# Softmax maxima as a row of the second pass's contraction, and two passes issued together in half steps of two strips

## The chip, the cores and the metric

The kernel runs on one core of one Trainium2 chip. The metric is the device time of one execution in microseconds, given as the median of several runs; a profiled execution gives the trace that the text reads. The engines are called as in the profile: PE (TensorE, with PEld for its weight loads), DVE (VectorE), ACT (ScalarE), POOL (GpSimd) and SP (the queue that issues most DMAs).

## The reference

Two layers of a network on 8 batches of 512 tokens with 256 channels, all in f32. The first layer is a multi-query attention (16 heads of 16 channels; one key head and one value head shared by all) and a top-64 mixture of 16 experts; the second is a linear attention and a coupled three-cycle network. Only the first attention matters here:

```python
q = (x @ Wq + bq).reshape(Bx, Tx, HEADS, HD)          # 16 heads of 16
k = (x @ Wk + bk)[:, :, None, :]                      # one head for all
v = (x @ Wv + bv)[:, :, None, :]
q, k = _apply_rope(q, ...), _apply_rope(k, ...)
att = jnp.einsum('bthd,bThd->bhtT', q, k) / math.sqrt(HD)
att = jnp.where(causal, -jnp.inf, att)
att = jax.nn.softmax(att, axis=-1)
out = jnp.einsum('bhtT,bThd->bthd', att, v).reshape(Bx, Tx, Cx)
return out @ Wo + bo
```

`x` there is a layer-normed and modulated input, and the result is added to `x` with a gate per batch and channel.

## The kernel before, in words

**Strips.** Keys and queries are kept transposed, channels on partitions. `qT[:, g]` holds 8 heads of 16 channels on 128 partitions (g = 0, 1). The 32 partitions 32j to 32j+31 are strip j: they hold two heads, an even one (p = 0) and an odd one (p = 1). `kT[:, p]` is the shared key, repeated on all partitions, with zeros on the 16 rows of the other head, so that one matmul over the 32 rows of strip j scores one head. Four strips lie in four row groups of PE, so four such matmuls can run at once, each into its own PSUM bank.

**Two passes.** Softmax needs the row maxima before it exponentiates. The first pass, `maxima(b)`, scores queries against keys with the queries on the output partitions: `L646` are the scores, `L654` adds a mask to each diagonal block of 128 x 128 by a bf16 matmul with the identity, and DVE takes maxima over stretches of 128 keys (`L668`, and `L661` where a bank holds blocks of two heads). The second pass, `heads_of(b)`, scores again with the keys on the output partitions: `L725` are the scores, `L733` subtracts the maxima by a further bf16 matmul, ACT exponentiates (`L740`) into `e`, POOL zeroes what lies above the diagonal (`L744`), and `values(n)` (`L710`) multiplies `e` with the values and a column of ones.

**Rounds.** Causal blocks of 512, 384, 256 and 128 columns are packed so that a round fills a 512-column bank: per g five rounds, `rounds`, of which three hold two blocks. A pass thus has ten rounds per batch, each of four strips, and takes or fills four banks in a round.

**The maxima's way.** `L675` reduces the partial maxima, `L679` and `L682` split them into three bf16 parts whose sum is the f32 number (three casts, two subtractions), four bf16 transposes (`L688`) turn them, ACT copies them to `mT` (`L691`). `minus` is a matrix of zeros and minus ones that picks, in the contraction of `L733`, the three rows that belong to a head.

**Order of the work.** The order on every engine is that in which the program emits instructions. `Steps.run()` goes round a set of lanes (Python generators) in order of rank, each lane emitting up to its next `yield`. A batch is one lane: `made_ready(b)` (norm, q, k, v, rope, transposes `L606`, `L616`), `maxima(b)`, `heads_of(b)`, `finished(b)` (transposes `L776` and `L791`, output product `L805`, norm, router logits `L831`). A new batch starts every 15 steps, so in the steady state four batches are under way: `finished(b)`, `heads_of(b+1)`, `maxima(b+2)`, `made_ready(b+3)`. A step holds one round of each pass, whole: first the four strips of the second pass, then the four of the first. The ranks are 0 for `finished`, 1 for `made_ready`, 2 for `heads_of`, 3 for `maxima`.

**Banks.** All PSUM tiles come from one pool of eight banks (`net.mm()`). A tile can be written when the reader of the bank's last tile is through. First-pass strips are released by DVE, second-pass strips by ACT, transposes and projections by either.

After the first attention come the experts (`experts_side`), the second layer's attention, and the coupled network; no line of theirs is changed, except that the second attention's lanes are counted in half steps too.

## Time and profile before

| what | value |
|---|---|
| median of 6 runs | 1192.93 us (1190.21 to 1195.59) |
| the profiled execution | 1191.77 us, its span 1190.0 us |
| mean granted clock of PE | 0.973 |
| PE busy | 1101.7 us (93%) |
| DVE busy | 711.1 us (60%) |
| ACT busy | 555.0 us (47%) |
| POOL busy | 498.2 us (42%) |
| matmuls of the first pass, L646 | 1024 records, 136.0 us busy |
| matmuls of the second pass, L725 | 1024 records, 106.5 us busy |
| mask, L654 | 512 records, 42.9 us busy |
| subtraction of the maxima, L733 | 512 records, 43.5 us busy |
| DVE maxima, L668 and L661 | 320, 198.4 us busy, 683 ns mean |
| exponentials, L740 | 320, 164.7 us busy, 604 ns mean |

An f32 matmul leaves two records (two loads, two matmuls), a bf16 one leaves one. PE's work is pipelined: the records of one line overlap those of the next, so that the busy times of lines add up to more than the span that they take; start-to-start distances are what one pays. A matmul that stands before the array and waits for a bank can count as busy. "Idle before" a group tells how long its engine stood still and whose work ended it.

### The profile page before, as it was taken

How to read it: one execution, taken by the hardware profiler on the slowest of the kernel's cores; microseconds unless marked ns; L12 is line 12 of the kernel's file. 1: busy time of each engine (PE TensorE's matmuls, PEld its weight loads, DVE VectorE, ACT ScalarE, POOL GpSimd, SP SyncE). 2: the span in 40 equal slices, each digit the busy share in tenths (PEclk: the TensorE clock that was granted, in tenths of full speed). 3: DMA queues.
4: the chain of work that ended last, by engine and by line, in shares of the span. 5: the costliest groups of instructions: out<-in, count | busy, mean ns of one | idle time of the engine just before them, and what ended most of it. 6: DMA issues, size and time to landing. Idle time of an engine off the chain costs nothing. (4 is left out here: it accounts for less than half of the span.)

```text
span 1190.0 us, 22170 instructions
## 1 busy us (share of the span) xinstructions
PE 1101.7 (93%) x8942; PEld 709.9 (60%) x8942; DVE 711.1 (60%) x1463; ACT 555.0 (47%) x1024; POOL 498.2 (42%) x539
## 2 busy tenths in 40 slices
PE   4879999999999999989898898799999988999996
PEld 3545666666666665478676776466666665444433
DVE  4967675767666666822652223666667655556765
ACT  2145656565656546724332344344444323555444
POOL 3022334344443424477787787355556444000000
PEclk8889999999999999999999999899999998999998
DMA  6200010000000001378758854400000000000202
GB/s 212 69 10 2 2 28 25 28 25 28 25 28 25 28 27 35 115 234 253 186 89 203 222 80 58 104 7 6 6 6 6 6 2 1 0 1 1 71 0 72
DMA packets 67975, 69.11 MB, mean 58 GB/s; under 512 B 10216, under 2 KB 64544, under 8 KB 67872
## 3 DMA queue, kind: packets, MB, share of 16 engines
q1 hardware_dynamic: 55024, 49.32, 13.3%
q0 software_dynamic: 12288, 16.79, 8.4%
q8 instruction: 71, 1.16, 0.4%
q10 hardware_dynamic: 560, 1.58, 0.4%
q14 instruction: 32, 0.26, 0.1%
HBM read 46.38 MB, written 21.01 MB: 57 GB/s over the span
## 5 line engine op out<-in xcount | busy, mean ns | idle before, releaser
L740 ACT ACTIVATE e<-mm 128x512 f32<-128x512 f32 x320 | 164.7, 604 | 103.1 <-PE mm L733 99.2
L668 DVE TENSOR_REDUCE pm<-mm 128x4 f32<-128x512 f32 x256 | 158.7, 683 | 84.1 <-PE mm L654 83.8
L744 POOL TENSOR_SCALAR_AFFINE_SELECT e<-e 128x512 f32<-128x512 f32 x128 | 80.3, 645 | 252.3 <-ACT e L740 252.3
L646 PE MATMUL mm<-kT,qT 32*128 32x128 f32 (+3 forms) x1024 | 136.0, 467 | 1.5 <-DVE o_tok L783 1.4
L1134 POOL DMA_INDIRECT xs<-y,slot x64 | 102.3, 1598 | 31.8 <-issue 13.3
L725 PE MATMUL mm<-qT,kT 32*128 32x128 f32 (+3 forms) x1024 | 106.5, 465 | 0.0
L646 PEld LDWEIGHTS mm<-kT,qT 32*128 32x128 f32 x1024 | 75.3, 189 | 45.0 <-DVE pm L668 10.9
L1642 PE MATMUL mm<-g,cn_w 128*128 128x512 f32 x192 | 98.3, 625 | 0.0
L710 PE MATMUL mm<-e,vaug 128*32 128x512 f32 (+3 forms) x1024 | 77.2, 436 | 3.9 <-POOL e L744 2.5
L725 PEld LDWEIGHTS mm<-qT,kT 32*128 32x128 f32 x1024 | 57.2, 184 | 26.6 <-issue 10.6
L1035 POOL DMA_INDIRECT tok<-xg,gidx x64 | 63.5, 993 | 19.1 <-issue 16.0
L1685 DVE SCALAR_TENSOR_TENSOR m<-th,slope,g 128x512 f32<-128x512 f32 x48 | 34.0, 747 | 58.8 <-ACT th L1678 58.8
L1462 POOL TENSOR_SCALAR_AFFINE_SELECT am<-am 128x1024 f32<-128x1024 f32 x32 | 44.1, 1381 | 55.5 <-ACT am L1460 55.5
L1111 PE MATMUL mm<-ew,hid 128*128 128x256 f32 x256 | 63.8, 394 | 1.0 <-ACT hid L1100 0.8
L1100 ACT ACTIVATE hid<-mm,eb 128x512 f32<-128x512 f32 x32 | 22.0, 686 | 91.2 <-PE mm L1091 91.2
L1098 DVE TENSOR_SCALAR hid<-mm,eb 128x512 f32<-128x512 f32 x32 | 24.0, 750 | 67.1 <-PE mm L1091 67.0
L1091 PE MATMUL mm<-hid,ew 128*128 128x256 f32 x256 | 61.5, 384 | 0.0
L1091 PE MATMUL mm<-tokT,ew 128*128 128x256 f32 x256 | 60.8, 380 | 0.1
L1116 DVE SCALAR_TENSOR_TENSOR y<-mm,eb,gb 128x512 f32<-128x512 f32 x32 | 23.9, 745 | 61.5 <-PE mm L1111 61.5
L1290 PE MATMUL mm<-hT,w1qkv 128*128 128x512 f32 x128 | 58.8, 604 | 0.0
L1642 PEld LDWEIGHTS mm<-g,cn_w 128*128 128x128 f32 x192 | 33.6, 195 | 41.7 <-issue 40.0
L1460 ACT COPY am<-mm 128x512 f32<-128x512 f32 x64 | 34.3, 591 | 44.5 <-PE mm L1448 30.7
(245 smaller groups left out, 2208.2 us busy)
## 6 DMA issues: line engine op xcount, KB each, us to landing
ew<-in_L_ffn_w SPq DMA_DIRECT2D x72, 256.0 KB, 5.9
x<-in_L_attn_x SPq DMA_DIRECT2D x8, 512.0 KB, 8.2
xs<-x SPq DMA_DIRECT2D x8, 512.0 KB, 4.9
xg<-xh SPq DMA_DIRECT2D x8, 512.0 KB, 4.1
x<-xs SPq DMA_DIRECT2D x8, 512.0 KB, 9.3
out<-res SPq DMA_DIRECT2D x16, 256.0 KB, 2.2
ga_row<-gate_a SPq DMA_DIRECT2D x16, 128.0 KB, 3.1
mod_row<-rows SPq DMA_DIRECT2D x16, 128.0 KB, 4.0
```

Source lines behind the costliest of these rows:

```text
L646: nc.tensor.matmul(strips[j][:, at : at + nk], qT[rows_of(j), g, i * P : (i + 1) * P], kT[rows_of(j), p, :nk], start=(n == 0), stop=False, ...
L668: nc.vector.tensor_reduce(pm[:, j, 2 * g + p, first : first + 4], strips[j].rearrange("q (a k) -> q a k", k=P), AX.X, ALU.max,)
L710: nc.tensor.matmul(av[32 * j : 32 * j + 32, c * P :], va[:, c, :], e[:, j, at : at + T - c * P], start=(a == 0), stop=(a == 3), skip_group ...
L725: nc.tensor.matmul(strips[j][:, at : at + T - c * P], kT[rows_of(j), p, c * P : (c + 1) * P], qT[rows_of(j), g, c * P :], start=(n == 0), ...
L740: nc.scalar.activation(e[:, j, :], strips[j], AF.Exp, scale=scale)
L744: nc.gpsimd.affine_select(out=own, in_=own, compare_op=ALU.is_ge, fill=0.0, base=0, pattern=[[0, 4], [1, P]], channel_multiplier=-1,)
L1035: self.net.nc.gpsimd.indirect_dma_start(out=tok[:, n, :], out_offset=None, in_=self.net.xg[half], in_offset=bass.IndirectOffsetOnAxis(ap=s ...
L1091: nc.tensor.matmul(ps[:, o * C : (o + 1) * C], w[i][n][:, k, o * P : (o + 1) * P], src[:, k, :], start=(k == 0), stop=(k == 1),)
L1111: nc.tensor.matmul(ps[:, n * C : (n + 1) * C], hid2[i][:, k, n * P : (n + 1) * P], w[i][2][:, k, :], start=(k == 0), stop=(k == 1),)
L1134: nc.gpsimd.indirect_dma_start(out=net.xs[2 * half + n], in_=y[i][:, n, :], in_offset=None, out_offset=bass.IndirectOffsetOnAxis(ap=self.s ...
L1290: nc.tensor.matmul(ps, w[:, k, n * P : (n + 1) * P], hT[:, k, :], start=(k == 0), stop=(k == 1))
L1642: nc.tensor.matmul(ps, w1[:, k, o * P : (o + 1) * P], g[k][bb], start=(k == 0), stop=(k == 1),)
```

## The change

Three things are changed together, in the first attention alone.

1. **The maxima become a row of the contraction.** Queries are kept once per head of a strip: `qT[g][:, p]` now has zeros on the 16 rows of the other head, as `kT[:, p]` has. On those rows `kT[:, p]` gets a minus one at the first of them (a bias of the ACT instruction that writes it). In the first pass this row meets a zero. Afterwards the maxima, in f32, are transposed (`L732` of the new kernel, eight f32 transposes in place of four in bf16) and added by DVE into that row of `qT[g][:, p]` (`L737`, four `scalar_tensor_tensor`). The second pass then needs no subtraction: `L733` of the old kernel is gone, and with it the bf16 parts, `mT` and its copy. `kT` and `qT` have two buffers instead of three.

2. **Masks of a bank are added by one matmul** instead of one per block (`hide`).

3. **Half steps.** A lane may yield a list of groups of matmuls instead of emitting them. `Steps.run()` collects these lists and emits them group by group: in one half step two strips of the second pass and two of the first, in different row groups, then the masks. Both passes walk the same list, `ORDER`, in which `None` is a place where the second pass does `values(n)` and the first nothing. All other lanes move every second half step. Batches start every 30 half steps.

Besides, the adds of the output bias and the two products with the modulation rows on POOL are split by tiles of 128 tokens, and `values(n)` is emitted in two halves.

```diff
     def run(self):
+        step = 0
         while self.starters or self.lanes:
             self.starters = [s for s in self.starters if next(s, self) is not self]
+            together = []
             for at in sorted(self.lanes, key=lambda at: at[:2]):
+                if step % at[3] != at[4] % at[3]:
+                    continue
                 self.now = at
-                if next(at[2], self) is self:
+                got = next(at[2], self)
+                if got is self:
                     self.lanes.remove(at)
+                elif got is not None:
+                    together.append((at, got))
+            for groups in itertools.zip_longest(*(got for _, got in together), fillvalue=()):
+                for issue in itertools.chain(*groups):
+                    issue()
+            for at, _ in together:
+                self.now = at
+                if next(at[2], self) is self:
+                    self.lanes.remove(at)
+            step += 1
...
-        kT = fp.tile([P, 2, T], F32, name="kT", bufs=3)
+        kT = fp.tile([P, 2, T], F32, name="kT", bufs=2)
...
         for p in range(2):
-            nc.scalar.activation(kT[:, p, :], ps, AF.Copy, scale=even_odd[:, p : p + 1])
+            nc.scalar.activation(
+                kT[:, p, :], ps, AF.Identity, bias=minus[:, 1 - p : 2 - p],
+                scale=even_odd[:, p : p + 1],
+            )
...
-            nc.scalar.copy(qT[:, g, :], ps)
+            q = fp.tile([P, 2, T], F32, name=f"qT{g}", bufs=2)
+            for p in range(2):
+                nc.scalar.activation(q[:, p, :], ps, AF.Copy, scale=even_odd[:, p : p + 1])
...
+    ORDER = (0, 1, 2, 3, None, 4, 5, None, 6, 7, 8, None, 9)
...
+            for js in ((0, 1), (2, 3)):
+                strips, groups = scores(g, blocks, js)
+                yield groups
+                for j in js:
...
         for i in range(NT):
-            nc.vector.tensor_reduce(mx[:, i], pm[:, :, :, blocks_of[i]], AX.X, ALU.max)
-        left = mx
-        for r in range(3):
-            part = m3[:, :, :, r : 12 : 3]
-            nc.vector.tensor_copy(part, left)
-            if r < 2:
-                rest = fp.tile([P, NT, 4, 4], F32, name=f"rest{r}")
-                nc.vector.tensor_tensor(rest, left, part, ALU.subtract)
-                left = rest
-            yield
-        mT = fp.tile([P, T], BF16, name="mT")
-        ps = net.mm(BF16)
-        for i in range(NT):
-            nc.tensor.transpose(
-                ps[:, i * P : (i + 1) * P], m3[:, i].rearrange("p j s -> p (j s)"), net.identb
-            )
-        nc.scalar.copy(mT, ps)
+            for p in range(2):
+                nc.vector.tensor_reduce(
+                    mx[:, i, :, :, 1 - p, 0],
+                    pm[:, :, p:4:2, blocks_of[i]].rearrange("q j g k -> q g j k"), AX.X, ALU.max,
+                )
+        yield
+        for g in range(2):
+            ps = net.mm()
+            for i in range(NT):
+                nc.tensor.transpose(
+                    ps[:, i * P : (i + 1) * P], mx[:, i, g].rearrange("q j p e -> q (j p e)"),
+                    net.ident,
+                )
+            for p in range(2):
+                nc.vector.scalar_tensor_tensor(
+                    qT[g][:, p, :], ps, even_odd[:, 1 - p : 2 - p], qT[g][:, p, :],
+                    ALU.mult, ALU.add,
+                )
+            yield
         yield
...
-                for p, a, at in blocks:
-                    c = chunk_of[a]
-                    for j in range(4):
-                        nc.tensor.matmul(
-                            strips[j][:, at : at + T - c * P],
-                            minus[rows_of(j), 2 * g + p, :], mT[rows_of(j), c * P :],
-                            start=False, stop=True, skip_group_check=True,
-                        )
...
+            for js in ((2, 3), (0, 1)):
+                strips, groups = scores(g, blocks, js)
+                yield groups
+                for j in js:
+                    nc.scalar.activation(e[:, j, :], strips[j], AF.Exp, scale=scale)
```

## The prediction

> **What bounds the kernel now.** I read the page's slices first, because the change touches only the first attention, and then its groups.

> ```profile
> PE   4879999999999999989898898799999988999996
> DVE  4967675767666666822652223666667655556765
> PEclk8889999999999999999999999899999998999998
> ```

> Slices of 29.75 us: from the fourth to the seventeenth TensorE is full while VectorE stands at 5 to 8 tenths. The transposes of the maxima (L688) begin at 69.0 for batch 0 and at 467.8 for batch 7, so seven batches pass in 398.8 us, 57.0 each. The windows view, cut at the period, repeats to a hundredth (columns: window, length, then busy time and count of PE, PEld, DVE, ACT, POOL, then clock):

> ```profile
> 234.00:292.50 58.50, 58.09 (x617) 36.29 (x617) 39.87 (x85) 33.64 (x65) 23.91 (x30) 1.00 0.09 27
> 292.50:351.00 58.50, 58.10 (x617) 36.30 (x617) 39.87 (x85) 33.64 (x65) 23.91 (x30) 1.00 0.08 27
> ```

> So a batch is 58.5 us of TensorE; VectorE and ScalarE have 18.6 and 24.9 us to spare, and the clock is full. But a waiting matmul counts as busy, so the timeline of TensorE decides how much of that is work:

> ```profile
> 301.57 0.40 PE L654 MATMUL mm<-maskb,identb 128*128 128x128 bf16 x4
> 301.90 1.22 PE L725 MATMUL mm<-qT,kT 32*128 32x384 f32 x16
> 302.87 0.46 PE L733 MATMUL mm<-mT,minus 32*128 32x384 bf16 x8
> ...
> 316.27 0.40 PE L654 MATMUL mm<-maskb,identb 128*128 128x128 bf16 x4
> 316.50 0.39 PE L791 MATMUL mm<-ident,o_tok 128*128 128x128 f32 x2
> ...
> 340.19 0.40 PE L733 MATMUL mm<-mT,minus 32*128 32x256 bf16 x8
> 340.40 2.03 PE L646 MATMUL mm<-kT,qT 32*128 32x512 f32 x8
> 342.37 0.40 PE L654 MATMUL mm<-maskb,identb 128*128 128x128 bf16 x4
> ```

> I count from start to start, since tails overlap. A round of the second pass (L725, four strips at once) takes 301.90 to 302.87 = 0.97 us. The same work in the first pass (L646) takes 340.40 to 342.37 = 1.97 here. The ten rounds of this batch take 1.20, 1.45, 2.15, 1.08, 2.09, 0.97, 1.08, 1.97, 1.97 and 2.36 us in the first pass, 16.3 in all, some 0.6 of it interleaved second-pass work, against 10.1 for the second pass: **5.6 us of waiting per batch**. It waits for banks that VectorE empties four at a time:

> ```profile
> 301.84 2.48 DVE L668 TENSOR_REDUCE pm<-mm 128x4 f32<-128x512 f32 x4 [0.65 <-PE mm L654]
> 307.91 2.48 DVE L668 TENSOR_REDUCE pm<-mm 128x4 f32<-128x512 f32 x4 [0.84 <-PE mm L654]
> ```

> Each reduction occupies VectorE 0.62 us; both lines start as soon as the mask matmuls are through.

> **The change, per batch of 58.5 us, TensorE first.**

> *Removed: the matmuls that subtract the maxima (L733).* 64 per batch. A round with one block has four, about 0.30 us; one with two blocks eight, 0.39 us (302.87 to the next start 303.26). 4 × 0.30 + 6 × 0.39 = **−3.6 us**. All on the path: TensorE is full.

> *Added: transposes of the maxima in f32.* Eight instead of four bf16 ones. Four f32 transposes take 0.50 (L776, as above a start-to-start distance), four bf16 ones 0.32 (L688, 296.57 to 296.89): 2 × 0.50 − 0.32 = **+0.7 us**.

> *Merged: mask matmuls.* 64 of 128 columns become 16 of 128 and 24 of 256, the same columns. Four of 128 take 0.23 (316.27 to 316.50), eight 0.46 (307.59 to 308.05): the cost is the columns, so **0**.

> *Moved: masks after every half step.* The mask uses the whole array, the scores 32-row strips. Four masks followed by another full-array job last 0.23, followed by strips 0.33 (301.57 to 301.90): a change of shape costs 0.10. Now there are 13 entries into strips per batch, after the change 20, and as many exits: 14 × 0.10 = at most 1.4; exits often cost nothing (324.08 to 325.05 is the bare 0.97), so between 0.7 and 1.4; I take **+1.3**. [...]

> *Pairing.* In the new order a half step issues two strips of the second pass (row groups 64 to 127, say) and two of the first (0 to 63), block by block with equal sizes, so four still run at once and scores keep 2 × 10 × 0.97.

> Without any waiting TensorE would need 58.5 − 5.6 − 3.6 + 0.7 + 1.3 = **51.3 us**.

> *VectorE.* Gone are three casts and two subtractions, 3 × 0.24 + 2 × 0.23 = 1.4. Added are four more small reductions (L675, four in 0.50: 0.4) and four 128x512 scalar_tensor_tensor from PSUM; the trace shows one of 0.75 (L1116), so 3.0. 39.9 − 1.4 + 3.4 = **41.9**. ScalarE: two more 0.58 copies, less mT's 0.5: 34.3. GpSimd's 2.36 us adds are cut in four; nobody waits for them. No DMA is added. kT and qT have two buffers instead of three: the new kT waits for the last second-pass round two batches back, behind exponentials that need the same matmuls, so 0.

> *What is left of the waiting.* Eight banks; a half step takes four and its side job one or two, so half step k+1 needs what VectorE released from k−1. A half step is TensorE about 1.25 (scores, two masks, a shape change), VectorE 1.24. Side jobs unbalance it in two places. Where BN statistics (1.0), cosd (1.43) and kd (0.6) fall on five half steps in a row, VectorE needs 5 × 1.24 + 3.0 = 9.2 against 6.3: some 2.5 us late even after the one half step of slack. At the start of a batch the last scalar_tensor_tensors, BN statistics (2.0) and four o_tok (4 × 0.63) make 1.4 us more. I take **3.9**, against 5.6 now; bounds 0 (VectorE's sum is 9.4 below TensorE's) and 7.2 (its bursts eat the whole gain).

> *The seam.* Both passes now walk the same list, so four half steps between batches hold no scores. The chain there: last mask, two reductions (1.45), wo_g and bo_g (0.94), eight small reductions (0.9), transposes (0.7), two scalar_tensor_tensors (1.5) = 5.5 us to the first usable queries. TensorE has meanwhile the k and q transposes, values(3), both transposes of maxima and the logits, 6 us. Cost 0.3, in the 3.9.

> Period: 51.3 + 3.9 = 55.2, **−3.3** (bounds −7.2 and 0). Seven such intervals, three of them without some lane, so I count 4 × 3.3 + 3 × 3.0 = **−22**.

> *Ends.* Batch 0's first pass runs alone, two strips at a time: a pair costs what four do, since a lone f32 matmul of 512 columns takes 2 × 0.51 (L1642, 98.3 us for 192). That is up to +9.7 of TensorE, but there VectorE is busy 27.6 of 31.5 us, so it is the bound: between 0 and +8, I take +2. Batch 7's second pass alone loses L733 (−3.6) and pairs only where no other matmul lies between half steps (up to +9.7): −3.6 to +6, taken +1. Together **+3**.

> Sum: −22 + 3 = −19. The profiled execution took 1191.8 (span 1190.0, 1.8 around it), 1.2 below the median of the six runs: 1172.8 on its scale, 1174 on the median's; as the later layers run the same instructions I leave them as they are and say 1173.

> **The rivals.**

> *The waits go (1147).* Two reductions at a time release banks every 1.24 instead of 2.48 us. Then 51.3 per batch: 7 × −7.2 + 3 = −47; allowing some residue, 1147 to 1158. For it: VectorE is only 82% full. Against: the two crowded places.

> *VectorE becomes the bound (1191).* All 7.2 are eaten: 1190 to 1196 with the ends. For it: the present 5.6 at 68% load; VectorE's load rises to 76%.

> *Slower: the seam is exposed (1210).* The place is the wait of the transposes of the maxima, which stand in TensorE's queue ahead of half of values(3) and the logits. If VectorE reaches the chain late, its 5.5 us lie open: +5.5 − 3.3 = 2.2 per batch, 15 in all, with the ends 1210. It decides from 3.3 us of idle TensorE per seam. The trace has such a place, batch 0, where nothing covers:

> ```profile
> 66.07 1.09 PE L606 MATMUL mm<-ident,kd 128*128 128x128 f32 x4 [5.24 <-DVE kd L594]
> ```

> and the windows view (first pair of numbers 4.00 us: TensorE busy; the last three: clock, DMA share, GB/s):

> ```profile
> 70.00:74.00 4.00, 4.00 (x23) 1.50 (x21) 0.00 (x0) 1.95 (x5) 0.00 (x0) 0.57 0.00 0
> ```

> 5.24 us idle, and then a granted clock of 0.57. [...] Against it: the 6 us of cover.

> *It does not pair (1309).* If strips of two passes did not overlap, scores would double: 20 × 0.97 = 19.4 more per batch, 136 in seven. Against: today's four are also separate instructions into separate banks.

> **Numbers.** Forecast 0.60 (1158 to 1186), waits gone 0.18, VectorE bound 0.10 (of this 0.03 faster, 0.04 same, 0.03 slower), seam 0.09, no pairing 0.03. Six runs spread over 0.45%, so about 0.3% (3.6 us) can be told from no change. Faster 0.60 + 0.18 + 0.03 = 0.81, same 0.04, slower 0.15. Range: from inside the second case to the top of the third, 1151 to 1191; outside lie the seam, no pairing and the lower part of the second case, 0.2.

> **What would show it.** Right: a period near 55 us; L733's successor absent; scores of both passes in mixed bursts of about 1 us; VectorE near 42 of 55; first-pass matmuls still waiting where cosd and kd fall; no half clock at the seams. Wrong: a period of 51 (waits gone) or 58 (VectorE at 90% around the reductions), TensorE idle over 3 us before the transposes of the maxima, or bursts of 2 us.

## The result, and the profile after

The changed kernel takes 1200.39 us (median of 20 runs, 1192.21 to 1203.92) against 1192.95 us (median of 46, 1189.54 to 1198.53): ratio 1.0047, interval 1.0033 to 1.006. It is slower by half a per cent, where a gain of 1.7% was forecast, and lies above the range. Within the changed kernel the time goes with the mean granted clock: four runs at 0.965 to 0.966 took 1192.2 to 1193.1 us, those at 0.954 to 0.956 took 1198.9 to 1203.9 us; no trace of any of the four was kept, so where they gain is not known. The profiled execution took 1198.88 us, span 1197.2, clock 0.956 (before: 0.973).

The page's slices (29.9 us each now), in the rows that were read before:

```profile
PE   4999999999999999979898999799999988999996
DVE  4577968586777777722552223666667655556765
PEclk8579999999999999999899999899999998999998
```

TensorE looks as full as before. The news is in the second and third digits of the last row, 5 and 7 where 8 and 8 stood, and in VectorE's second digit, 5 for 9. The middle of the first attention is better than before (windows view, cut at the new period; columns as above):

```profile
188.40:245.10 56.70, 56.55 (x535) 31.85 (x534) 42.23 (x88) 35.72 (x66) 25.70 (x39) 1.00 0.09 27
245.10:301.70 56.60, 56.45 (x534) 31.75 (x532) 42.12 (x88) 35.63 (x66) 25.70 (x39) 1.00 0.09 28
```

58.5 us per batch have become 56.65, with VectorE at 42.2 (41.9 forecast). Three stretches of the profiled spans, cut at the first and last score of the second pass (L725 before, L777 after), hold the whole difference:

| stretch | before | after | difference |
|---|---|---|---|
| start to the first score of the second pass | 70.4 | 89.4 | **+19.0** |
| from there to the last one | 428.8 | 414.5 | **-14.3** |
| from there to the end | 690.8 | 693.3 | +2.5 |

So a gain of the expected kind is there, and is lost again before the second pass has begun. There batch 0's first pass runs alone. The windows view of that place, before:

```profile
40.00:50.00 10.00, 10.00 (x101) 6.09 (x97) 9.65 (x18) 1.77 (x3) 0.00 (x0) 1.00 0.01 2
50.00:60.00 10.00, 10.00 (x89) 6.47 (x82) 9.83 (x26) 0.00 (x0) 0.82 (x1) 1.00 0.01 3
```

and after:

```profile
40.00:50.00 10.00, 10.00 (x38) 4.56 (x36) 5.38 (x10) 2.07 (x4) 1.55 (x4) 0.50 0.00 0
50.00:60.00 10.00, 10.00 (x46) 4.68 (x47) 5.01 (x13) 0.78 (x1) 0.00 (x0) 0.50 0.00 0
60.00:70.00 10.00, 10.00 (x32) 5.18 (x29) 5.57 (x12) 0.78 (x1) 0.00 (x0) 0.50 0.09 26
```

TensorE is busy all the time in both. Before, VectorE is at 9.65 and 9.83 of 10 at full clock: it is the bound, as the prediction had it. After, VectorE is half idle, and the clock stands at 0.50 without a break from 25 to 70 us. The timeline of TensorE after shows what runs at that clock:

```profile
47.87 2.08 PE L674 MATMUL mm<-kT,qT 32*128 32x512 f32 x4
49.88 0.39 PE L684 MATMUL mm<-maskb,identb 128*128 128x128 bf16 x2
50.20 2.08 PE L674 MATMUL mm<-kT,qT 32*128 32x512 f32 x4
52.21 0.39 PE L684 MATMUL mm<-maskb,identb 128*128 128x128 bf16 x2
```

A half step of two strips takes 2.33 us (47.87 to 50.20), of which VectorE uses two reductions (1.29 us, L717 from 50.20 on). Both kernels come to this place with a low clock (0.60 and 0.75 before, 0.50 and 0.50 after, in the windows from 25 and from 30 us), and in both TensorE has little to do from 20 to 35 us (busy 5.17 of 15.00 us before, 6.86 after). Before, it is at 1.00 from 40 us on, to the end of this pass. After, it opens only between 71 and 72 us (0.72 in the window of that microsecond, 0.50 in those ahead of it, 1.00 from 72 us on), towards the end of a long product over the whole array (L582: q, k and v of the next batch):

```profile
66.35 6.68 PE L582 MATMUL mm<-wqkv,hT 128*128 128x288 f32 x16
72.96 1.14 PE L674 MATMUL mm<-kT,qT 32*128 32x384 f32 x8
74.03 0.39 PE L684 MATMUL mm<-maskb,identb 128*128 128x256 bf16 x2
```

From then on the scores of the same two strips take 1.07 us (72.96 to 74.03) where they took 2.01 (47.87 to 49.88): twice the clock, half the time.

**The steady state after**, in the timeline of TensorE: a half step without waiting, then one that waits.

```profile
263.53 0.70 PE L777 MATMUL mm<-qT,kT 32*128 32x512 f32 x2
263.54 0.70 PE L674 MATMUL mm<-kT,qT 32*128 32x512 f32 x2
264.06 0.59 PE L777 MATMUL mm<-qT,kT 32*128 32x512 f32 x2
264.08 0.59 PE L674 MATMUL mm<-kT,qT 32*128 32x512 f32 x2
264.60 0.28 PE L684 MATMUL mm<-maskb,identb 128*128 128x128 bf16 x2
...
292.67 0.70 PE L777 MATMUL mm<-qT,kT 32*128 32x512 f32 x2
293.09 0.69 PE L674 MATMUL mm<-kT,qT 32*128 32x512 f32 x1
293.20 0.59 PE L777 MATMUL mm<-qT,kT 32*128 32x512 f32 x2
293.62 1.19 PE L674 MATMUL mm<-kT,qT 32*128 32x512 f32 x3
294.74 0.28 PE L684 MATMUL mm<-maskb,identb 128*128 128x128 bf16 x2
```

The first takes 263.53 to 264.60 = 1.07 us for two strips of each pass, so the passes do run together. The second takes 292.67 to 294.74 = 2.07: the second pass's strips go, the first pass's wait for banks that VectorE still holds. It is the half step that cosd delays, as the timeline of VectorE shows:

```profile
291.15 1.28 DVE L602 TENSOR_TENSOR cosd<-qkv,rope 128x1088 f32<-128x1088 f32 x1
292.35 2.48 DVE L710 TENSOR_REDUCE pm<-mm 128x4 f32<-128x512 f32 x4
```

kd runs on VectorE only at 296.56, and no half step waits behind it (the next one, at 298.54, takes 1.08).

### The profile page after: what moved, and what is told of

Read it like the earlier page. It is cut to its first block, busy times and chain, and to the rows that moved or that the text cites. A ratio compares the mean times of both kernels' runs of the same rounds, so it can differ in the third digit from the quotient of the medians.

```text
span 1197.2 us, 20955 instructions
## 1 busy us (share of the span) xinstructions
PE 1118.8 (93%) x8270; PEld 687.6 (57%) x8270; DVE 727.5 (61%) x1487; ACT 570.1 (48%) x1032; POOL 510.6 (43%) x610
## 5 line engine op out<-in xcount | busy, mean ns | idle before, releaser
L799 ACT ACTIVATE e<-mm 128x512 f32<-128x512 f32 x320 | 172.1, 598 | 105.8 <-PE mm L777 89.2
L674 PE MATMUL mm<-kT,qT 32*128 32x384 f32 (+3 forms) x1024 | 208.6, 487 | 0.1
L717 DVE TENSOR_REDUCE pm<-mm 128x4 f32<-128x512 f32 x256 | 162.8, 682 | 61.4 <-PE mm L684 60.2
L777 PE MATMUL mm<-qT,kT 32*128 32x384 f32 (+3 forms) x1024 | 180.3, 465 | 0.0
L804 POOL TENSOR_SCALAR_AFFINE_SELECT e<-e 128x512 f32<-128x512 f32 x128 | 86.0, 691 | 186.5 <-ACT e L799 186.4
L1186 POOL DMA_INDIRECT xs<-y,slot x64 | 102.1, 1596 | 34.3 <-issue 13.7
L674 PEld LDWEIGHTS mm<-kT,qT 32*128 32x128 f32 x1024 | 98.9, 194 | 22.6 <-issue 9.1
L777 PEld LDWEIGHTS mm<-qT,kT 32*128 32x128 f32 x1024 | 83.1, 184 | 45.8 <-issue 22.0
L1087 POOL DMA_INDIRECT tok<-xg,gidx x64 | 63.7, 995 | 19.4 <-issue 15.9
L1514 POOL TENSOR_SCALAR_AFFINE_SELECT am<-am 128x1024 f32<-128x1024 f32 x32 | 44.1, 1380 | 56.4 <-ACT am L1512 56.4
L684 PEld LDWEIGHTS <-identb 128*128 128x128 bf16 x320 | 18.4, 98 | 73.2 <-issue 65.9
L684 PE MATMUL mm<-maskb,identb 128*128 128x256 bf16 (+1 forms) x320 | 58.0, 265 | 0.0
```

Source lines behind the costliest of these rows:

```text
L674: nc.tensor.matmul(strips[j][:, at : at + nk], qT[g][rows_of(j), p, i * P : (i + 1) * P], kT[rows_of(j), p, :nk], start=(n == 0), stop=Fal ...
L684: nc.tensor.matmul(strips[j].rearrange("q (n k) -> q n k", k=P)[:, own], net.identb, maskb.unsqueeze(1).to_broadcast([P, len(ends), P]), s ...
L717: nc.vector.tensor_reduce(pm[:, j, 2 * g + p, first : first + 4], strips[j].rearrange("q (a k) -> q a k", k=P), AX.X, ALU.max,)
L777: nc.tensor.matmul(strips[j][:, at : at + T - c * P], kT[rows_of(j), p, c * P : (c + 1) * P], qT[g][rows_of(j), p, c * P :], start=(n == 0 ...
L799: nc.scalar.activation(e[:, j, :], strips[j], AF.Exp, scale=scale)
L804: nc.gpsimd.affine_select(out=own, in_=own, compare_op=ALU.is_ge, fill=0.0, base=0, pattern=[[0, 4], [1, P]], channel_multiplier=-1,)
```

## The experiments

All times are given with the ratio to the kernel before on the same chip and its 95% interval. After is the changed kernel, before the old one; a bracket in a heading names the kernel that is edited. Three dots in a diff stand for lines left out.

**1. Four strips at once in batch 0's first pass (after).** If the start is what is lost, this returns it.

```diff
-            for js in ((0, 1), (2, 3)):
+            for js in ((0, 1, 2, 3),) if b == 0 else ((0, 1), (2, 3)):
...
                 yield
+                if b == 0:
+                    yield
```

> The changed kernel, but in batch 0 the first pass issues all four strips of a round in one half step and rests in the next, as long as no second pass runs beside it. Both theories of the late start (clock: two strips at a time keep the granted clock at 0.5, pairing: two strips stream as long as four at any clock) expect the first scores of the second pass near 71 us instead of 89, a clock of 1.0 from 40 to 60 us, and the whole at 1200 - 18 = 1182, with the steady period unchanged at 56.7. A third theory (the longer way of the maxima and the half steps themselves make the start late) expects at least 1195.

Measured: 1180.57 us, ratio 0.9898 (0.9882 to 0.9913). The first score of the second pass comes at 69.6 instead of 89.4; the period stays 56.65. Its windows:

```profile
40.00:50.00 10.00, 10.00 (x79) 6.14 (x78) 9.90 (x23) 3.12 (x6) 0.00 (x0) 1.00 0.01 2
50.00:60.00 10.00, 9.41 (x65) 5.46 (x64) 9.93 (x20) 0.00 (x0) 3.84 (x3) 0.98 0.15 28
```

Full clock, and VectorE the bound again. One line of the order is worth 18 us (0.0149 of 1193). But this edit changes two things, the clock and the two halves that a pair takes one after the other; the next one parts them.

**2. Pairs as in after, but the idle strips scored as well (after).** In batch 0 each half step also scores the two other strips, into banks that nobody reads: more work for TensorE and for the banks, none for VectorE.

```diff
             strips = {j: net.mm() for j in js}
+            idle = [j for j in range(4) if j not in js] if b == 0 else []
+            strips.update({j: net.mm() for j in idle})
...
-                [functools.partial(score, j, n, *block) for j in js]
+                [functools.partial(score, j, n, *block) for j in (*js, *idle)]
```

> The changed kernel with work added: in batch 0's first pass the two strips whose row groups would be idle in a half step are scored too, into banks that nobody reads, and again in their own half step. If it is the clock, the added matmuls open it (granted clock 1.0 from about 40 us) and the kernel becomes 10 to 17 us faster than the changed one, 1184 to 1190, though it does twice the scores there. If it is pairing alone, the added strips run beside the others at no cost and no gain: 1200, clock still 0.5 until 70 us. If full arrays of work simply add up, 1210 or more.

Measured: 1185.56 us, ratio 0.9937 (0.9921 to 0.9954); the first score of the second pass at 73.8. Its windows:

```profile
40.00:50.00 10.00, 10.00 (x106) 5.34 (x108) 8.41 (x16) 2.85 (x5) 1.11 (x3) 1.00 0.01 2
50.00:60.00 10.00, 10.00 (x88) 6.16 (x80) 8.53 (x23) 0.78 (x1) 1.67 (x2) 1.00 0.09 28
60.00:70.00 10.00, 10.00 (x105) 5.48 (x100) 9.88 (x15) 0.00 (x0) 1.12 (x2) 1.00 0.01 2
```

128 more matmul records than after (8398 against 8270), and 13 us less by the ratios, because the clock opens. Of the 19.8 us between after and the first experiment, 15.6 (89.4 - 73.8) are thus the clock, and 4.2 (73.8 - 69.6) what pairs cost at full clock. These 4.2 are a net figure: batch 0's first pass alone takes 38.2 us here and 30.9 in experiment 1, 7.3 more, and 3.4 come back in the chain behind it, where the clock is 1.00 here (70 to 75 us) and 0.50 to 0.52 in experiment 1 (60 to 70 us).

**3. The converse: pairs in batch 0's first pass of the kernel before.** No row of maxima, no half steps elsewhere.

```diff
             for blocks in rounds:
-                strips = [net.mm() for _ in range(4)]
+                for js in ((0, 1), (2, 3)) if b == 0 else ((0, 1, 2, 3),):
+                    strips = {j: net.mm() for j in js}
...
-                    for j in range(4):
+                        for j in js:
```

> The kernel before, but in batch 0 alone the first pass issues its strips two at a time, each pair with its masks. If pairs without a partner keep the clock at 0.5, the second pass begins some 15 us later than the 70 us of before and the kernel takes 1205 to 1212. If only the doubled streaming counts (10 x 0.97 us more of TensorE, partly under VectorE's 27.6 of 31.5 us), the clock reaches 1.0 by 45 us and the kernel takes 1194 to 1199.

Measured: ratio 1.0146 (1.0117 to 1.0176). Three executions took 1210.46 to 1211.89 us; a fourth took 3251.57 us, for which no run shows a cause, and is not counted. This is the first case of the expectation: the first score of the second pass comes at 90.9 instead of 70.4, and the period is still 58.5. Its windows:

```profile
40.00:50.00 10.00, 10.00 (x51) 4.64 (x43) 5.24 (x11) 0.17 (x1) 0.00 (x0) 0.50 0.00 0
50.00:60.00 10.00, 10.00 (x42) 5.03 (x40) 4.94 (x8) 0.78 (x1) 0.00 (x0) 0.50 0.01 2
```

The whole loss, made in a kernel that has nothing else of the change.

**4. The row of maxima alone, in whole steps (before).** Part 1 of the change, with the emission order of before.

```diff
-            nc.scalar.copy(qT[:, g, :], ps)
+            q = fp.tile([P, 2, T], F32, name=f"qT{g}", bufs=2)
+            for p in range(2):
+                nc.scalar.activation(q[:, p, :], ps, AF.Copy, scale=even_odd[:, p : p + 1])
+            qT.append(q)
...
+                nc.vector.scalar_tensor_tensor(
+                    qT[g][:, p, :], ps, even_odd[:, 1 - p : 2 - p], qT[g][:, p, :],
+                    ALU.mult, ALU.add,
+                )
...
-                        nc.tensor.matmul(
-                            strips[j][:, at : at + T - c * P],
-                            minus[rows_of(j), 2 * g + p, :], mT[rows_of(j), c * P :],
-                            start=False, stop=True, skip_group_check=True,
-                        )
```

> The kernel before with the first part of the change alone: maxima as a row of the contraction, queries once per head, whole steps of four strips of one pass as before, masks per block. By the sum of the prediction a period loses 3.6 for the subtraction and gains 0.9 for the f32 transposes, and the waits stay: 55.8 us, 7 x 2.7 = 19 less, 1174, with the start as before. If the half steps bring something in the steady state, its period is longer than the changed kernel's 56.7; if they cost something there, it is shorter. If the longer chain of the maxima shows at the batch seam, 57 to 59.

Measured: 1182.45 us, ratio 0.9906 (0.9893 to 0.9919), where 1174 was expected. One period in the windows view:

```profile
228.80:286.00 57.20, 56.21 (x559) 35.36 (x558) 41.86 (x88) 34.55 (x67) 24.32 (x30) 1.00 0.09 27
```

57.2 instead of 58.5: of the 3.6 us of L733, the scores, waits included, take 1.8 back (27.7 us per period from start to start, against 25.9), and the f32 transposes 0.7. The half steps save a further 0.55 (57.2 to 56.65). So the row is most of the gain, and the half steps, as they stand, cost more at the start than they bring in seven batches. Even with the start mended they bring nothing that the timed runs can tell: experiment 1 stands at 0.9898, this one at 0.9906.

**5. Half of VectorE's maxima (after).** This leaves out a part of the computation. The reductions read only the first 64 keys of every 128, so the maxima are of half the keys: is VectorE what is still waited for?

```diff
-                            strips[j].rearrange("q (p a k) -> q p a k", p=2, k=P),
+                            strips[j].rearrange("q (p a k) -> q p a k", p=2, k=P)[..., : P // 2],
...
```

> The changed kernel, with the maxima taken over the first 64 of every 128 keys only (part of the computation left out), so that a reduction on VectorE is about 0.27 us shorter, 10.8 per batch. If the remaining waits of the scores (25.8 us per batch against 21.6 of bare rounds) are for VectorE, the period falls from 56.7 to 53 or less. If they are changes of the array's shape and TensorE's own queue, it stays above 56.

Measured: 1179.35 us, ratio 0.9886 (0.9852 to 0.992).

```profile
234.00:288.50 54.50, 54.33 (x534) 30.70 (x533) 32.08 (x87) 35.63 (x66) 25.10 (x39) 1.00 0.09 29
```

10 us less of VectorE give 2.15 us of period, between the two cases of the expectation; the waits of the scores go from 4.25 to about 2.0. The start is late all the same (first score of the second pass at 85.0), though VectorE has half as much to reduce: it is not VectorE that holds it.

**6. No masks in the first pass (after).** The mask matmuls, with their changes of shape, are left out.

```diff
...
-            groups.append([functools.partial(hide, j) for j in js])
```

> The changed kernel without the mask matmuls of the first pass (the maxima then range over later keys too), to measure what changing the array's shape costs. A period has 4.66 us from mask starts to next starts, and a bare half step of scores takes 1.075 where it is followed by masks. If leaving the strips costs 0.10, half steps that follow each other directly take 0.97 and the period falls by 4.7 and up to 2 more, to 50 to 52, unless the waits for VectorE grow. If only the columns of the masks count (64 x 0.053 = 3.4), it falls to 53.

Measured: 1177.29 us, in a single execution.

```profile
228.00:284.20 56.20, 55.16 (x494) 32.85 (x492) 42.60 (x88) 35.50 (x65) 25.74 (x40) 1.00 0.10 28
```

4.66 us of masks gone, 0.4 gained, where 3.7 or more were expected: five half steps in a row now take 9.49 us, 1.9 each instead of 1.07, and wait for VectorE. In the steady state the two engines stand in balance; either alone, relieved, runs into the other. What an exit from the strips costs could not be told apart here, since a bare half step still takes 1.07 to 1.08.

The time fell by far more than seven periods explain, because this run starts on time: the first score of the second pass comes at 72.2 instead of 89.4. Its windows at the start:

```profile
40.00:50.00 10.00, 10.00 (x60) 5.30 (x60) 8.72 (x23) 3.00 (x6) 0.69 (x3) 0.66 0.00 0
50.00:60.00 10.00, 9.96 (x64) 6.22 (x60) 9.93 (x20) 0.63 (x1) 3.52 (x3) 1.00 0.10 30
```

Batch 0 is still issued in pairs, but with no mask between them pairs run side by side in different row groups: two half steps take 2.02 us here (34.42 to 36.44, 12 records at the clock of 0.50), where one took 2.01 in after. So by this run it was not the pairs by themselves that kept the clock at 0.50, but pairs held apart by masks over the whole array.

**7. Four strips at both ends (on experiment 1; batch 7's second pass too).**

```diff
-            for js in ((2, 3), (0, 1)):
+            for js in ((2, 3, 0, 1),) if b == B - 1 else ((2, 3), (0, 1)):
...
+                if b == B - 1:
+                    yield
```

> The kernel of the four strips in batch 0 (1180.6), and the second pass of the last batch too issues four strips in one half step and rests in the next. From the transposes of the maxima to the last second-pass score batch 7 took 31.7 us in the kernel before and 37.4 in that of the four strips. If pairs that stream as long as four strips cost this, it falls to 32 or 33 and the time to 1176. If VectorE's choice of the experts' tokens or GpSimd's selects set the pace there, nothing changes.

Measured: 1178.86 us, ratio 0.9891 (0.987 to 0.9912). From the transposes of batch 7's maxima to the last score: 33.8 us against 37.4 in experiment 1. Of these 3.6 us 1.9 arrive at the end of the span (1178.3 to 1176.4), and in the timed runs they cannot be told from nothing (0.9891 against 0.9898).

**8. cosd, kd and qd one step later (experiment 7).** The crowded place that the prediction named is moved to the next step.

```diff
+        yield
         heads = qkv[:, :, : C + HD].rearrange("p i (h e) -> p i h e", e=HD)
...
         yield
-        yield
```

> The kernel with four strips at both ends, and in addition the rope products (cosd, kd, qd) one step later, so that kd falls where no scores are and qd two half steps before the seam. Waits of 0.77 and 1.0 us per period stand in the two half steps after cosd and kd. If they come from VectorE's queue there, the period falls from 56.7 to between 55.0 and 55.8 and the whole by 5 to 8 us. If qd then delays the chain of the maxima by its 1.13 us, the period stays at 56.7 or rises.

Measured: 1179.64 us, ratio 0.988 (0.9859 to 0.9901), period 56.4. The wait at the half step behind cosd is gone (2.07 becomes 1.07), the one ahead of it (0.77) stays, and half of `values` at the seam takes 2.53 instead of 1.84. The wait is moved, not removed.

**9. The seam's product wo_g and bo_g earlier (experiment 7).**

```diff
             if q is None:
+                if not oT:
+                    wg, bg = net.gated_by(pool, wo, bo, ga)
                 yield from values(len(oT))
...
-        wg, bg = net.gated_by(pool, wo, bo, ga)
```

> The kernel with four strips at both ends, and VectorE's two gate products (wo_g, bo_g, 1.5 us per batch) moved from the seam to the first place without scores. If VectorE's queue sets the waits that are left, the chain of the maxima starts 1.5 us earlier, the wait ahead of the transposes of the maxima and the first waits of the next batch shrink, and the period falls from 56.7 by 0.7 to 1.5, the whole by 5 to 10 us (1169 to 1174). If TensorE's own work and shape changes set the period, it stays at 56.7 and 1179.

Measured: 1178.33 us, ratio 0.9867 (0.9849 to 0.9884), period 56.35. The period is shorter by 0.3 us, where 0.7 to 1.5 was expected; the waits of 0.77 and 1.0 stay.

**10. cosd on GpSimd (experiment 9).** 1.28 us less for VectorE at the crowded place.

```diff
-        nc.vector.tensor_tensor(
+        nc.gpsimd.tensor_tensor(
             cosd, heads,
```

> The same, and in addition the product with the cosines (1.2 us of VectorE per batch, in the crowded place of half steps 18 to 20) on GpSimd. If VectorE's queue sets the waits there (0.77 and 1.0 us), the period falls by another 0.5 to 1.5 us, the whole to 1160 to 1170. If GpSimd, on which the product takes longer and stands ahead of the selects, holds up the keys or the exponentials, the period stays or rises.

Measured: 1185.91 us, ratio 0.993 (0.9916 to 0.9944), period 58.0. The view of waits, for one period (engine and what waits, whose work it waits for: us, times, longest):

```profile
DVE kd L610 <- POOL cosd L602: 4.3, 1, 4.3
PE mm L761 <- POOL e L808: 2.3, 1, 2.3
```

cosd takes 2.5 us there. VectorE now waits 4.3 us for it, and the selects on `e` that queue behind it on GpSimd come late to `values` (L761), for which TensorE stands still 2.3 us. The wait it was aimed at did go.

## Why the prediction was wrong, point by point

**The step that failed: "Batch 0's first pass runs alone ... there VectorE is busy 27.6 of 31.5 us, so it is the bound: between 0 and +8, I take +2."** It was +19. The step was worked out at the clock of before: 2 x 0.51 for a lone matmul, at most +9.7 of TensorE. Experiment 2 shows that at full clock it held: there the second pass begins 3.4 us later than before (73.8 against 70.4), within its bounds. What it did not ask is whether half as many strips would still open the clock. They did not: 15.6 us more, at 0.50. Experiments 1 to 3 show it from three sides: four strips in after (-18 us), pairs with the idle strips filled in (-13), pairs in before (+17, from the ratio 1.0146). Experiment 6, without the masks between the pairs, is a fourth: the second pass begins 17.2 us earlier. The prediction had a half clock in its list, but only for an idle TensorE at the seam, and looked for it under "idle over 3 us". Here TensorE was busy 10.00 of 10.00 us in each of the three windows from 40 to 70 us, and the clock stood at 0.50 all the same.

**The steady period: right in sign and mechanism, half the size.** -1.85 instead of -3.3. Start to start over the lines of one period:

| term | forecast | measured |
|---|---|---|
| subtraction gone (L733) | -3.6 | -3.6 |
| f32 transposes of the maxima | +0.7 | +0.85 |
| shape changes | +1.3 | +2.0 |
| waits, 5.6 before | -1.7 (3.9 left) | -1.4 (4.25 left) |
| other lines | 0 | +0.3 |

The mis-sized term is the shape changes. Entries cost what was forecast (the masks' lines take 0.70 more), but a bare half step takes 1.075 us where a round took 1.01 on average, 20 x 0.065 = 1.3 in all; the prediction had taken the exits as nearly free. That these 1.3 us are the exits is argued from the count, not shown. For it: the same four strips of the second pass took 0.97 before, where L733, in strips too, came next, and 1.07 in experiment 4, where a transpose over the whole array does (234.91 to 235.98). Against it: the 0.97 ahead of a mask that the prediction quotes (324.08 to 325.05).

**The waits: about right in place, and in size partly by luck.** Of the 4.25 us, 2.48 stand at the start of a batch (1.4 forecast) and 1.77 in the crowded place (2.5 forecast): 0.77 behind the batch norm's statistics, which put off the reductions from 288.90 to 289.98, and 1.0 behind cosd; kd costs nothing. The two misses cancel in the sum. The 2.5 also did not follow from its own terms: 9.2 - 6.3 is 2.9, and less one half step of 1.25 it is 1.7, near the 1.77 measured. The rival by which they go is out, and so is the one by which VectorE is the bound. Experiments 5 and 6 say why: TensorE and VectorE are in balance. VectorE's load came out at 42.2 instead of 41.9: in that sum 3 x 0.24 + 2 x 0.23 is 1.2, not 1.4, and with it 42.1 was forecast.

**The seam: right.** No half clock in the steady state (1.00 in both periods shown above), and 0.3 us to be won (experiment 9). The rival that ended slower had the right side for a cause that did not occur. **Pairing: right**, 1.07 us for four strips of two passes.

**Batch 7's second pass: +4.7 instead of +1** (31.7 to 36.4 from the transposes of its maxima to the last score), within the bounds -3.6 to +6. The clock is 1.00 there, in every window from 465 to 505 us. The way from the first of these transposes to the first score grew by 1.7 (1.5 to 3.2 us), and the scores, from first to last, by 2.9 (30.3 to 33.2). The pairs are what lengthens the scores: with four strips at once experiment 7 takes 3.6 back, and in experiment 4 they take 29.3. But that is 0.9 less than before, not the 3.6 that the loss of L733 was to bring there, and experiment 4, whose way to the first score is 5.9 us, needs 35.3 in all without any pair.

**Later layers.** "I leave them as they are" missed 3.2 us: from the last product wo_g, oTd to the end it is 660.6 us before and 660.2 in experiment 3, but 663.8 after, 663.4 in experiment 1 and 661.8 in experiment 4 (row alone); 666.8 in experiment 9. So not the half steps alone; the cause stays open.

In sum, for the profiled executions: -14.3 in the middle (forecast -22 + 1 = -21), +19.0 at the start (+2), +2.5 behind it. The middle holds the seven intervals between the transposes of the maxima, batch 7's second pass, and a little at its beginning. The intervals went from 398.6 to 380.1 us (the 398.8 of the prediction ends at the last of batch 7's four transposes), -18.5 of the forecast -22. That the sum comes so near is luck: the five in the middle gave -8.7 (forecast about -16), the first and the last -5.2 and -4.6 (-3.0 each). No run shows why these two gained more. With the start as it was, the change is worth 1.0% (experiment 1), with small mends 1.3% (experiment 9); the row alone 0.9%.

## What to carry to other kernels

## What the hardware showed that was not expected

- Matmuls of two 32-row strips with masks of 0.39 to 0.61 us between them, from 31.6 us on and with TensorE busy 5.00 of 5.00 us in every window from 35 us, left the clock at 0.50 until 71 us; with four strips it opened within some 5 us (in experiment 1 scoring begins at 31.2 us, and the clock is 0.93 over 35 to 40 us). 64 further matmuls (128 records) into unread banks made the kernel 13 us faster. That it is the filled rows that count, and not some other property of these matmuls, is inferred from experiments 1, 2, 3 and 6.
- Once open, the clock stayed open under pairs: in the rest of batch 0's first pass of after (1.00 in the window from 75 to 80 us), and in batch 7's second pass of after, with other products between, every window from 475 to 505 us shows 1.00. How much work opens it, and how little keeps it open, was not measured.
- A pair of strips takes as long as four: 1.07 us for a half step of two and two, 1.07 (72.96 to 74.03) for two alone at a clock of 1.00, and 2.01 (47.87 to 49.88) for two alone at 0.50.
